# Strassen's seven products for the first layer's down projection, and the branch moved to other banks and hooks

## The chip, the core and the metric

The kernel runs on one core of one Trainium2 chip. The metric is the device time of one launch in microseconds (us), a median over runs. The core has a matrix engine (PE, whose weight loads the profile shows apart as PEld), a vector engine (DVE), an activation engine (ACT), a general engine (POOL) and a queue engine (SP) that starts most of the data transfers (DMA). SBUF is the working memory. PSUM is the small memory that the matrix engine writes to: eight banks of 128 partitions by 512 float32 numbers.

## The reference

Two residual layers act on 2048 tokens of width 512 (two sequences of 1024), all in float32. The part that is changed is layer 0:

```python
xn = layernorm(x)
x = x + attn_ref(xn) + ffn_ref(xn)
# attn_ref: a second layernorm, a recurrence of rank 8 along the sequence,
#           and a small feed-forward of rank 8 behind it ("the branch")
# ffn_ref:
hidden = silu(xn @ W1.T) * (xn @ W3.T)        # 2048 tokens x 2048 hidden
hidden = fwht(hidden)                         # Walsh-Hadamard transform
out = hidden @ W2.T                           # 2048 tokens x 512
```

Layer 1 follows with causal attention of 16 heads and a feed-forward of the same size whose hidden values are thinned to two of every four.

## The kernel before

The Hadamard transform is applied to `W2` once, in SBUF (`fwht_rows`, `fwht_step`), so that layer 0's feed-forward is gate, up and down products alone. The 2048 tokens are four blocks of 512; two blocks are handled together. A *unit* is the gate and the up projection of one pair of blocks for 256 of the 2048 hidden columns: layer 0 has 16 units, `n` 0 to 15, eight for blocks 0 and 1 and then eight for blocks 2 and 3.

`gate_up` (used by both layers) computes a unit by Strassen's algorithm in Winograd's form: seven calls of `products`, each of four matrix products of 128x128 by 128x512, and a few additions. It holds three pairs of PSUM banks, `pa`, `pb` and `pc`; the pairs change roles from unit to unit (`turns`). Between the seven blocks of products it calls `hook(0)` to `hook(6)`. All other work of layer 0 is hung on these hooks: the order of every engine's instructions is the order of the program text (`in_program_order`), and `put0(n, at, f, ...)` says that `f` is issued at hook `at` of unit `n`.

The down projection of a finished unit is not by Strassen. `down(n, i, half)` takes two of the four 128-token rows of block `i`, multiplies with the 256 hidden rows of `W2` into the two remaining PSUM banks (`two_banks`, tags `bank0` and `bank1`), and adds each bank into the residual `x1` on DVE (L634). `some_downs` takes these calls from a list at the hooks, 64 calls in all, from unit 3 on, and what is left comes behind the last unit:

```python
if n >= 3:
    some_downs((1, 1, 1, 1, 1, 1, 2)[at] if n < 5 else (1, 1, 0, 0, 1, 0, 1)[at])
```

The branch of each block is a chain of small steps on the same hooks and the same two banks: `load_again` (x once more, on SP), `branch_scale` (ACT, then POOL), `branch_out` (PE, then DVE L533, then POOL), `branch_add` (DVE statistics, POOL addition into `x1`), then for another block `ln_stats`, `ln_scale`, `ln_turn` (or `next_...`) with transposes on PE; `branch_mlp`, `branch_relu`, `branch_rank` prepare the rank-8 feed-forward, whose product is added inside the bank of the first `down` that comes after it (L628). `branch_scale` and `ln_scale` share one buffer (tag `z`).

Weights for gate and up come in tiles of 512 KB (`load_w13`), five buffers in all. POOL makes their four sums per unit (`combine_w`, L167 to L170), at hook 5 of the unit before.

Layer 1's feed-forward has the same `gate_up`, and its down projection is already by Strassen: for a group of two units and each half of the tokens, DVE makes sums of the hidden values (`down_hidden`, L1250 to L1253), POOL sums of the weights (`down_weights`), PE seven products (`down`, L1316) of four 128x128 by 128x256, and DVE (L1327, L1330), ACT (L1324) and POOL (`add_u2`, L1335) put them together in the residual.

## Time and profile before

| | us |
|---|---|
| Median of 3 runs | 1887.15 (1885.65 to 1887.47) |
| Profiled execution, its own time | 1882.42 |
| Its span in the trace | 1880.5 |
| PE busy | 1822.4 (97%) |
| DVE, POOL, ACT busy | 1067.7, 715.3, 464.8 |
| PE from the first layer-0 `down` to the first layer-1 product | 130.7 to 704.1 |

An entry such as `L621 PE MATMUL acc<-w2h,h ... x512 | 230.1, 594` means: line 621 of the kernel, engine, operation, tile written and tiles read, 512 instructions, 230.1 us busy, 594 ns for one from start to end. Each float32 matrix product of the program stands as two instructions in the trace. Matmuls overlap, so the distance from one to the next, not the length of one, is what a product costs; the chain of waits shows it. Idle time of an engine counts only where PE waits for it.

### The profile page before, as it was taken

The page shows a single profiled execution, that of the slowest core. Times are in us where ns is not written, and L with a number is a line of the kernel's source. Part 1 is how long each engine was busy: PE and PEld are TensorE (multiplying, and loading weights), DVE is VectorE, ACT ScalarE, POOL GpSimd, SP SyncE. Part 2 cuts the span into 40 slices and gives each one's busy share as a digit, 9 for nine tenths or more (in the row PEclk, how much of TensorE's full clock was granted, in tenths as well). Part 3 has the DMA queues.
Part 4 walks back from the last instruction along what each step waited for, and adds up shares of the span by engine and source line. Part 5 has one row for each costly group of instructions (what it writes and reads, how often), then busy time and mean ns, then how long its engine had stood idle before and what let it go on. Part 6 is the DMA issues. An engine that isn't in the chain of part 4 may idle for free.

```text
span 1880.5 us, 17921 instructions
## 1 busy us (share of the span) xinstructions
PE 1822.4 (97%) x6964; PEld 844.2 (45%) x6964; DVE 1067.7 (57%) x1424; ACT 464.8 (25%) x659; POOL 715.3 (38%) x635
## 2 busy tenths in 40 slices
PE   7999999999999999999999999999999999999997
PEld 4444444444444444333333333334455555555553
DVE  3674443334443235656565657652768678668664
ACT  2321121112221102343433343421212211221210
POOL 4222233113432101376667666732243344244310
PEclk9999999999999999999999999999999999999999
DMA  6121111001101100000000100011101102201101
GB/s 236 40 79 34 34 34 34 23 23 34 51 23 34 34 6 23 1 12 12 3 10 12 33 14 1 23 45 34 34 24 55 56 23 79 79 23 50 40 0 45
DMA packets 29459, 68.04 MB, mean 36 GB/s; under 512 B 3392, under 2 KB 11584, under 8 KB 27840
## 3 DMA queue, kind: packets, MB, share of 16 engines
q1 hardware_dynamic: 28656, 66.61, 11.0%
q8 instruction: 55, 0.90, 0.2%
q10 hardware_dynamic: 720, 0.30, 0.1%
q14 instruction: 28, 0.23, 0.0%
HBM read 62.70 MB, written 4.19 MB: 36 GB/s over the span
## 4 chain that ended last, share of the span: by engine, by line
PE 88%; DVE 4%; POOL 4%; ACT 2%; issue 2%; DMA 0%; SPq 0%; ACTq 0%; DVEq 0%; POOLq 0%
PE p_a L177 20%; PE p_c L177 19%; PE acc L621 12%; PE d L1316 8%; PE pq L838 6%; PE m L890 4%; PE s L943 3%; PE o L985 3%; POOL acc L993 3%; PE pv L838 3%; PE dr L1372 2%; PE po L838 2%; PE w L1005 1%; PE pp L480 1%; DVE tops L898 1%
## 5 line engine op out<-in xcount | busy, mean ns | idle before, releaser
L993 POOL TENSOR_TENSOR acc<-acc,pt 128x1024 f32<-128x1024 f32 (+3 forms) x138 | 233.8, 1720 | 0.0
L621 PE MATMUL acc<-w2h,h 128*128 128x512 f32 x512 | 230.1, 594 | 3.1 <-DVE y L533 1.8
L898 DVE TENSOR_REDUCE tops<-m 128x2 f32<-128x1024 f32 (+2 forms) x192 | 180.9, 956 | 49.1 <-PE m L890 44.6
L634 DVE TENSOR_TENSOR x<-x,acc 128x512 f32<-128x512 f32 x128 | 86.1, 685 | 174.5 <-PE acc L621 137.9
L960 ACT ACTIVATE pt<-s 128x1024 f32<-128x1024 f32 (+3 forms) x160 | 115.1, 766 | 180.3 <-PE s L949 164.0
L621 PEld LDWEIGHTS acc<-w2h,h 128*128 128x128 f32 x512 | 96.5, 190 | 123.1 <-issue 115.0
L838 PE MATMUL pq<-xt,wqk 128*128 128x512 f32 x256 | 124.6, 615 | 0.8 <-ACT qk L854 0.8
L177 PE MATMUL p_a<-t_a,s_a 128*128 128x512 f32 x256 | 117.4, 603 | 2.0 <-DVE t_a L154 2.0
L177 PE MATMUL p_a<-xt,w 128*128 128x512 f32 x256 | 118.0, 604 | 0.7 <-ACT xt L134 0.7
L177 PE MATMUL p_c<-xt,s_c 128*128 128x512 f32 x256 | 115.2, 593 | 2.5 <-DVE e_c L221 1.4
L1335 POOL TENSOR_TENSOR x<-x,de 128x512 f32<-128x512 f32 x39 | 62.9, 1628 | 141.7 <-DVE x L1330 120.7
L177 PE MATMUL p_a<-xt,s_a 128*128 128x512 f32 x256 | 115.3, 593 | 0.0
L177 PE MATMUL p_c<-xt,gu 128*128 128x512 f32 x256 | 114.9, 592 | 0.0
L177 PE MATMUL p_c<-t_c,s_c 128*128 128x512 f32 x256 | 114.6, 592 | 0.0
L890 PE MATMUL m<-qk,qk 32*128 32x512 f32 (+3 forms) x768 | 107.5, 533 | 3.6 <-ACT acc L960 3.0
L897 DVE TENSOR_TENSOR m<-m,mask 128x256 f32<-128x256 f32 x128 | 54.7, 428 | 98.5 <-PE m L890 93.9
L943 PE MATMUL s<-qk,qk 32*128 32x512 f32 (+3 forms) x768 | 93.4, 532 | 3.2 <-ACT pt L960 2.3
L177 PEld LDWEIGHTS p_a<-t_a,s_a 128*128 128x128 f32 x256 | 48.7, 193 | 64.0 <-issue 62.4
L177 PEld LDWEIGHTS p_a<-xt,w 128*128 128x128 f32 x256 | 48.5, 193 | 64.3 <-issue 63.0
L965 POOL TENSOR_SCALAR_AFFINE_SELECT pt<-pt 128x256 f32<-128x256 f32 x112 | 48.6, 451 | 69.3 <-ACT pt L960 68.7
L985 PE MATMUL o<-pt,v 128*32 128x512 f32 (+3 forms) x640 | 70.1, 477 | 4.3 <-POOL pt L965 4.0
L838 PEld LDWEIGHTS pq<-xt,wqk 128*128 128x128 f32 x256 | 44.1, 189 | 66.6 <-issue 61.5
(227 smaller groups left out, 2762.1 us busy)
## 6 DMA issues: line engine op xcount, KB each, us to landing
w<-in_W SPq DMA_DIRECT2D x32, 512.0 KB, 3.6
gu<-in_gu SPq DMA_DIRECT2D x32, 512.0 KB, 3.6
wd<-in_down SPq DMA_DIRECT2D x8, 1024.0 KB, 4.9
x<-in_x SPq DMA_DIRECT2D x16, 256.0 KB, 4.2
w2h<-in_W2q SPq DMA_DIRECT2D x4, 1024.0 KB, 11.5
xr<-in_x SPq DMA_DIRECT2D x16, 256.0 KB, 2.6
wqk<-in_WqkvT SPq DMA_DIRECT2D x16, 256.0 KB, 3.2
out_x<-x SPq DMA_DIRECT2D x16, 256.0 KB, 2.0
```

The lines of the kernel that those rows point to most:

```text
L177: nc.tensor.matmul(pair[:, m, :], a[:, m, k, :], x[:, k, :], start=start and k == 0, stop=stop and k == 1, skip_group_check=True,)
L621: nc.tensor.matmul(bank, h[:, m, j * P : (j + 1) * P], w2h[:, :, 2 * (n % NU) + m, :], start=(m == 0), stop=(m == 1 and not up),)
L634: nc.vector.tensor_add(r, r, bank)
L838: nc.tensor.matmul(got[0], lhs(k), rhs(k), start=(k == 0), stop=(k == KC - 1))
L890: nc.tensor.matmul(pair[h // 2][:, h % 2, :e], q[rows, qt * P : (qt + 1) * P], k[rows, c * 512 : c * 512 + e], start=True, stop=True,)
L898: nc.vector.tensor_reduce(out=tops[u][:, c, qt, 2 * p : 2 * p + 2], in_=pair[p][:, :, :e], axis=mybir.AxisListType.X, op=ALU.max,)
L943: nc.tensor.matmul(pair[h // 2][:, h % 2, s:], k[rows, kt * P : (kt + 1) * P], q[rows, cols], start=True, stop=False,)
L960: nc.scalar.activation(pt[:, :, s:], pair[p][:, :, s:], AF.Exp, scale=1.0 / math.sqrt(HD))
L985: nc.tensor.matmul(po[rows, s:], v[:, rows], pts[h // 2][:, h % 2, s:], start=(kt == 0), stop=last, tile_position=(0, h * HD),)
L993: eng.tensor_add(acc[:, :, s:], acc[:, :, s:], pt[:, :, s:])
L1316: nc.tensor.matmul(out_[:, j, :], lhs[:, q, j * P : (j + 1) * P], rhs[:, q, :], start=m in (0, 1, 3, 4) and j == q == 0, stop=j == q == 1, ...
L1335: nc.gpsimd.tensor_add(r, r, held_d["u2"])
```

## The change

Layer 0's down projection is done by Strassen's algorithm as in layer 1, by a shared function, `down_by_seven`. The hidden values of two units lie in one tile (two such tiles). Each group of two units gives, for each half of the tokens, seven `product` calls at the hooks of the next two units, and DVE's `hidden` behind the first of them; one of the four sums overwrites its source (`in_place`). `down_weights` makes the weight sums on POOL; for the second pair of blocks one of them is still in place. The last group comes behind the last unit, its two halves taking turns, with two pairs of PSUM banks besides `bank0` and `bank1`.

The two single banks are now for the down products alone from unit 3 on. The branch takes the third pair, the one of `pb`: `gate_up` asks for `pb` only where it is used, and `two_banks` gives the same pair to the branch before and after it (`one_bank` gives its two halves to the calls of one hook). The steps of the branch are moved to later hooks, `mlp_out` is a step of its own with its own additions, and the branch of block 1 and the preparation of blocks 2 and 3 have other places. Smaller edits: four weight buffers in place of five (so four tiles are loaded at the start in place of five, and unit `n` is followed by the load for unit `n + 2`), two `row` buffers in place of three, the Hadamard matrix in the `rank` tiles, and a smaller scratch area.

```diff
-        pa, pb, pc = (ps_pair(f"p{m}_{name}", (turns + m) % 3) for m in range(3))
+        pa, pc = (ps_pair(f"p{m}_{name}", (turns + m) % 3) for m in (0, 2))
...
         def other_half():
+            pb = ps_pair(f"p1_{name}", turns % 3)
             products(pb, w1[:, :, 2:, :], x[:, 2:, :], start=True, stop=True)
             nc.vector.tensor_add(e[0], e[0], pb)
...
+    def down_by_seven(pool, hs, td, quarters_w, first_block, in_place=False):
+        sd, banks, e1, u2 = {}, {}, {}, {}
+        def quarters_h(n, half):
+            h = hs[n].rearrange("p (q two) b n -> p q two b n", two=2)
+            js = slice(half * TT // 2, (half + 1) * TT // 2)
+            return [h[:, :, c, i, js] for i in range(2) for c in range(2)]
...
+        def hidden(n, half, tags=("sd2", "sd3", "sd4")):
+            h11, h12, h21, h22 = quarters_h(n, half)
+            s3, s4 = (half_tile(tag, f"{tag}_{n}_{half}") for tag in tags[1:])
+            s2 = h11 if in_place else half_tile(tags[0], f"sd2_{n}_{half}")
+            sd[n, half] = s2, s3, s4
+            nc.vector.tensor_sub(s3, h11, h21)
+            nc.vector.tensor_add(h21, h21, h22)
+            nc.vector.tensor_sub(s2, h21, h11)
+            nc.vector.tensor_sub(s4, h12, s2)
...
+        def product(n, half, m, bank=None, tags=("de1", "de2")):
+            h11, h12, s1, h22 = quarters_h(n, half)
+            w11, t3, w21, w22 = quarters_w(n)
+            s2, s3, s4 = sd.get((n, half), (None,) * 3)
+            t1, t2, t4, t3 = (td[n] + [t3])[:4]
+            lhs, rhs = (
+                (h11, w11), (s2, t2), (h12, w21), (s1, t1), (s3, t3), (s4, w22), (h22, t4)
+            )[m]
+            if m in (0, 1, 3, 4):
+                if bank is None:
+                    bank = ps_bank(f"d{m}_{n}_{half}", (m + half) % 2)
+                banks[half, m % 2] = bank
+            out_ = banks[half, m % 2].rearrange("p (j d) -> p j d", j=2)
+            for j in range(2):
+                for q in range(2):
+                    nc.tensor.matmul(
+                        out_[:, j, :], lhs[:, q, j * P : (j + 1) * P], rhs[:, q],
+                        start=m in (0, 1, 3, 4) and j == q == 0, stop=j == q == 1,
+                        skip_group_check=True,
+                    )
+            if m == 0:
+                e1[half] = half_tile(tags[0], f"de1_{n}_{half}")
+                nc.scalar.copy(e1[half], out_)
+            elif m == 1:
+                u2[half] = half_tile(tags[1], f"de2_{n}_{half}")
+                nc.vector.tensor_add(u2[half], e1[half], out_)
+            else:
+                r = residual(n, half, *((0, 0), (1, 1), (1, 1), (0, 1), (1, 0))[m - 2])
+                nc.vector.tensor_add(r, r, out_)
+        def add_u2(n, half, *quarters):
+            for q in quarters:
+                r = residual(n, half, *q)
+                nc.gpsimd.tensor_add(r, r, u2[half])
+        def products_of(n, half):
+            for m in range(7):
+                yield product, n, half, m
+                if m == 1:
+                    yield add_u2, n, half, (0, 1), (1, 0)
+                if m == 4:
+                    yield add_u2, n, half, (1, 1)
+        return hidden, product, products_of
...
-            pool, tag, bufs = (res, "wqk", 2) if m % 5 in (2, 3) else (a, "w13", 3)
-            w13[m] = pool.tile([P, 2, KC, P], F32, tag=tag, name=f"w13_{m}", bufs=bufs)
+            pool, tag = (a, "w13") if m // 2 % 2 else (res, "wqk")
+            w13[m] = pool.tile([P, 2, KC, P], F32, tag=tag, name=f"w13_{m}", bufs=2)
...
             nc.sync.dma_start(out=w2h[:, q], in_=t["W2q"][q])
-            if q < 3:
+            if q < 2:
...
-            return a.tile([P, D], F32, tag="row", name=name, bufs=3)
+            return a.tile([P, D], F32, tag="row", name=name, bufs=2)
...
         def two_banks(name):
-            return [ps_bank(f"{name}_{n}", n) for n in range(2)]
-        turn = 0
+            if now < (3, 0):
+                return [ps_bank(f"{name}_{n}", n) for n in range(2)]
+            pair = ps_pair(name, turns % 3)
+            return [pair[:, n, :] for n in range(2)]
...
         def one_bank(name):
+            if now not in shared:
+                shared[now] = two_banks(name)
+            return shared[now].pop(0)
...
-            nxt = a.tile([P, P], F32, tag="had", name=f"had{step}", bufs=2)
+            nxt = a.tile([P, TT], F32, tag="rank", name=f"had{step}", bufs=2)[:, :P]
...
-        h0, downs = {}, []
-        def down(n, i, half):
-            h, js = h0[n, i], (2 * half, 2 * half + 1)
-            up = i in hf_t and (i, half) not in joined
-            if up:
-                joined.add((i, half))
-            banks = two_banks(f"acc_{n}_{i}_{half}")
+        def mlp_out(i, half):
             for bank, j in zip(banks, js):
-                for m in range(2):
-                    nc.tensor.matmul(
-                        bank, h[:, m, j * P : (j + 1) * P], w2h[:, :, 2 * (n % NU) + m, :],
-                        start=(m == 0), stop=(m == 1 and not up),
-                    )
-            if up:
-                for bank, j in zip(banks, js):
-                    rows = slice(32 * j, 32 * j + R + 1)
-                    nc.tensor.matmul(
-                        bank, hf_t[i][rows, j * P : (j + 1) * P], wup_aug[rows, :],
-                        start=False, stop=True,
-                    )
+                rows = slice(32 * j, 32 * j + R + 1)
+                nc.tensor.matmul(
+                    bank, hf_t[i][rows, j * P : (j + 1) * P], wup_aug[rows, :],
+                    start=True, stop=True,
+                )
             for bank, j in zip(banks, js):
                 r = x1[i][:, j, :]
                 nc.vector.tensor_add(r, r, bank)
-        joined = set()
-        def some_downs(n):
-            for _ in range(min(n, len(downs))):
-                down(*downs.pop(0))
...
+        def quarters_w(n):
+            return [w2_quarters[:, n % (NU // 2), c, e] for c in range(2) for e in range(2)]
+        def down_weights(n, m):
+            w11, w12, w21, w22 = quarters_w(n)
+            if m == 0:
+                td[n] = [
+                    a.tile([P, 2, D // 2], F32, tag=f"td{k}", name=f"td{k}_{n}") for k in (1, 2, 4)
+                ]
+            t1, t2, t4 = (v.rearrange("p q (s d) -> p q s d", s=2) for v in td[n])
+            if m == 0:
+                if n < NU // 2:
+                    nc.gpsimd.tensor_sub(w12, w22, w12)
+                nc.gpsimd.tensor_add(t2, w12, w11)
+            elif m == 1:
+                nc.gpsimd.tensor_sub(t1, w22, t2)
+            else:
+                nc.gpsimd.tensor_sub(t4, w21, t2)
+        down_hidden, down, products_of = down_by_seven(
+            a, h0, td, quarters_w, lambda n: n // (NU // 2) * 2, in_place=True
+        )
...
-            between.setdefault((n, at), []).append(what)
+            between.setdefault((n + at // 7, at % 7), []).append(what)
+        for n in range(NU - 1):
+            u = 2 * n + 2
+            places = [range(7), range(7, 14)]
+            if n == 0:
+                places = [(7, 8, 8, 9, 9, 10, 10), (11, 12, 12, 13, 13, 14, 14)]
+            elif n == 1:
+                places = [range(1, 8), (8, 9, 10, 11, 12, 13, 13)]
+            for half, at in enumerate(places):
+                for f, *args in products_of(n, half):
+                    if f == down:
+                        place = at[args[2]]
+                    put0(u, place + (f != down), f, *args)
+                    if f == down and args[2] == 0:
+                        put0(u, place, down_hidden, n, half)
+            for m, (k, f) in enumerate(((1, 1), (3, 1), (6, 1))):
+                at = places[1][k] + f
+                put0(u, at, down_weights, n + 1, m)
+        put0(2, 5, down_weights, 0, 0)
+        put0(2, 6, down_weights, 0, 1)
+        put0(2, 6, down_weights, 0, 2)
...
-            ((NU, 0), (NU, 2), (NU, 3)), ((NU, 3), (NU, 5), (NU, 6)),
+            ((6, 6), (7, 4), (7, 5)), ((8, 4), (8, 5), (8, 6)),
...
         for base in (0, NU):
             i, d = 2 * base // NU, base + (1 if base else 3)
             for m in range(4):
                 k = i + m // 2, m % 2
-                put0(d + m - 1, 6, load_again, *k)
-                put0(d + m, 0, branch_scale, *k)
-                put0(d + m, 2, branch_out, *k)
-                put0(d + m, 3, branch_add, *k)
+                put0(d + m, 0, load_again, *k)
+                put0(d + m, 2, branch_scale, *k)
+                put0(d + m, 3, branch_out, *k)
+                put0(d + m, 4, branch_add, *k)
                 k = (2 if base == 0 else 0) + m // 2, m % 2
-                put0(d + m, 3, next_stats if base else ln_stats, *k)
-                put0(d + m, 4, next_scale if base else ln_scale, *k)
-                put0(d + m, 5, next_turn if base else ln_turn, *k)
-            for m in range(2):
-                for at, f in ((0, branch_mlp), (1, branch_relu), (3, branch_rank)):
-                    put0(d + 2 * m + 2, at, f, i + m)
+                put0(d + m, 2, next_stats if base else ln_stats, *k)
+                put0(d + m, 5, next_scale if base else ln_scale, *k)
+                put0(d + m, 7, next_turn if base else ln_turn, *k)
+        for i, steps in enumerate((
+            ((5, 4), (5, 5), (6, 4), (6, 5), (8, 4)), ((7, 4), (7, 6), (8, 3), (9, 4), (10, 4)),
+            ((11, 4), (11, 5), (12, 4), (12, 5), (13, 4)),
+            ((13, 3), (13, 5), (14, 3), (14, 4), (14, 5)),
+        )):
+            for k, n in enumerate(steps):
+                if k < 3:
+                    put0(*n, (branch_mlp, branch_relu, branch_rank)[k], i)
+                else:
+                    put0(*n, mlp_out, i, k - 3)
...
-            put0(NU - 2, 3 + 3 * half, branch_in, 2, half)
-            put0(NU - 1, 1 + 2 * half, branch_in, 3, half)
-            put0(NU - 2 + half, 5, ln_spread, 2 + half)
+            put0(5 + half, 4, branch_in, 2, half)
+            put0(7, 3 + 2 * half, branch_in, 3, half)
+            put0(5 + half, 5, ln_spread, 2 + half)
...
-            for m in range(2):
-                h0[n, i0 + m] = a.tile(
-                    [P, 2, TT], F32, tag="h0", name=f"h0_{n}_{i0 + m}", bufs=6
-                )
+            if n % 2 == 0:
+                h = h0[n // 2] = a.tile([P, 4, 2, TT], F32, tag="h0", name=f"h0_{n}", bufs=2)
...
-                if n >= 3:
-                    some_downs((1, 1, 1, 1, 1, 1, 2)[at] if n < 5 else (1, 1, 0, 0, 1, 0, 1)[at])
...
-            downs += [(n, i0 + i, half) for i in range(2) for half in range(2)]
-            for m in (2 * n + 5, 2 * n + 6):
+            for m in (2 * n + 4, 2 * n + 5):
                 if m < 4 * NU:
...
-        some_downs(len(downs))
+        for f, *args in between.pop((2 * NU, 0), ()):
+            f(*args)
+        n, second_half = NU - 1, list(products_of(NU - 1, 1))
+        for step in products_of(n, 0):
+            for f, *args in (step, second_half.pop(0)):
+                if f == down and args[1] and args[2] in (0, 1, 3, 4):
+                    if args[2] in (0, 3):
+                        pair = ps_wide(f"d{args[2]}_{n}")
+                    f(*args, pair[:, args[2] in (1, 4), :], ("e2", "e3"))
+                else:
+                    f(*args)
+                if f == down and args[2] == 0:
+                    down_hidden(n, args[1], *([("", "e1", "t1")] if args[1] else []))
...
+        down_hidden, down, products_of = down_by_seven(
+            c_, hs, td, quarters_w, lambda n: 2 * units[2 * n][0]
+        )
...
+    nc = bacc.Bacc(
+        "TRN2", target_bir_lowering=False, num_devices=1, dynamic_dma_scratch_size=1024
+    )
```

## The prediction

> **What bounds the kernel now.** I read the page first. Its busy times say that PE is the engine to look at:
>
> ```profile
> PE 1822.4 (97%) x6964; PEld 844.2 (45%) x6964; DVE 1067.7 (57%) x1424; ACT 464.8 (25%) x659; POOL 715.3 (38%) x635
> ```
>
> That is an average, so next the windows of the stage that changes, from the first layer-0 down product to the first product of layer 1 (length, then PE, PEld, DVE, ACT, POOL busy, clock, DMA share, GB/s):
>
> ```profile
> 130.70:704.10 573.40, 570.33 (x1482) 257.55 (x1481) 224.51 (x390) 101.81 (x141) 147.38 (x124) 1.00 0.10 30
> ```
>
> PE is busy for 570 of 573 us at full clock; DVE has 39%, POOL 26%, DMA 10%. So what PE no longer does comes off the time, provided nothing makes it wait. The chain of waits, in order of time, gives the price of PE's work. First layer 0, then layer 1, whose down projection has the new form already:
>
> ```profile
> 134.29 3.43 PE p_a L177 x8
> 137.72 3.43 PE acc L621 x8
> ...
> 686.96 17.17 PE acc L621 x40
> 704.13 15.64 PE pq L838 x36
> ```
>
> ```profile
> 1355.39 1.73 PE d L1316 x8
> 1357.12 3.43 PE p_c L177 x8
> 1360.55 1.73 PE d L1316 x8
> ```
>
> Eight instructions with 512 columns take 3.43 us, eight with 256 take 1.73. Layer 1 repeats block and product every 5.16 us, so its interleaving leaves no gap there. Last, the groups of operations that will be exchanged, with shapes kept apart: DVE and POOL in layer 0, then in layer 1.
>
> ```profile
> L634 DVE TENSOR_TENSOR x<-x,acc 128x512 f32<-128x512 f32 x128 | 86.1, 685 | 174.5 <-PE acc L621 137.9 <-PE acc L628 36.7
> ...
> L545 POOL TENSOR_TENSOR x<-x,y 128x512 f32<-128x512 f32 x16 | 20.0, 1271 | 0.0
> ```
>
> ```profile
> L1330 DVE TENSOR_TENSOR x<-x,d 128x512 f32<-128x512 f32 x65 | 44.5, 684 | 46.9 <-PE d L1316 46.9
> ...
> L1250 DVE TENSOR_TENSOR sd<-h 128x512 f32<-128x512 f32 x13 | 13.8, 1059 | 0.0
> ...
> L1252 DVE TENSOR_TENSOR sd<-h 128x512 f32<-128x512 f32 x13 | 9.0, 692 | 0.4
> ```
>
> ```profile
> L1335 POOL TENSOR_TENSOR x<-x,de 128x512 f32<-128x512 f32 x39 | 62.9, 1628 | 141.7 <-DVE x L1330 120.7 <-DVE de L1327 21.1
> ...
> L1231 POOL TENSOR_TENSOR td<-wd 128x512 f32<-128x512 f32 x7 | 14.8, 2111 | 0.0
> ```
>
> **What the Trainium skill says.** "TensorE: Matmul & The Clock Gate", Back-to-back issue gap, has the gap between matmuls grow with the columns and almost no fixed part (its figures are for bf16). The trace agrees on the proportion: 3.43/8 = 0.429 and 1.73/8 = 0.216 us. Each product needs its own weight load, 190 ns in the trace, still under 216. "SBUF — State Buffer", section "SBUF: two separate sides", has DVE and POOL exclude each other for a whole instruction when DVE reads two operands from SBUF. The trace fits: L1250 takes 1059 ns where L1252, of the same shape, takes 692, and POOL additions range from 1271 to 2111.
>
> **The change, part by part.**
>
> 1. *Down products on PE.* Removed: 64 calls of 3.43 us = 219.6. Added: 8 groups x 2 halves x 7 products = 112 of 1.73 = 193.8. Minus 25.8 us, all on the path.
>
> 2. *The branch's feed-forward output* (`mlp_out`): the same 16 matrix products, no longer joined to a down call. PE 0; 16 more DVE additions of 0.685 = 11 us.
>
> 3. *DVE.* Removed 128 x 0.685 = 88. Added per half: four `hidden` operations at layer 1's lengths (1.06 + 0.69 + 0.69 + 1.09), one sum of 0.69, five residual additions of 0.684: 7.6 us, times 16 = 122. With part 2 DVE gets 45 us more, 270 in about 550 us: 49%. Hidden behind PE's blocks as long as each is in time. The critical one is s2, the third operation of `hidden`, for product 1. For most halves product 0 is at hook 0. Count from the end of block 7: PE does product 6 to 1.7, block 1 to 5.2, product 0 to 6.9, block 2 to 10.3, then product 1. DVE has its addition from `pc` at 1.4, the residual at 2.6, the last `h` at 3.3, two subtractions at 5.1, and s2 after product 0 at about 7.8. Slack 2.5 us: cost 0. In unit 3 the second half starts at hook 4, behind an addition of 1.22 and one of 0.68: s2 at 5.7 after block 5, product 1 wanted at 5.15. Cost 0.6, up to 2 if POOL holds DVE.
>
> 4. *ACT:* 16 copies of 0.58 = 9 us. One place matters: block 6 follows block 5 with one product (1.73) between, and needs ACT's copy of 1.01 from the same banks. Layer 1 runs exactly this. Cost 0.
>
> 5. *POOL.* 48 `add_u2` of 1.63 = 78 and 28 weight sums at 1.26 to 2.11, say 1.7, = 48: 273 in 550 us, 50%. The busiest are branch units: unit 5 has 17 additions and three short powers, about 25 to 28 us in 39. PE waits for POOL only at the second block of the next unit (`combine_w`); following POOL's order through units 5 and 9, its first sum is done some 8 us ahead. Cost 0.
>
> 6. *The third pair.* A `branch_out` at hook 3 needs the pair that `pb` had just left: DVE's addition ends about 1.45 us after block 4, the product between lasts 1.73. The two statistics of hook 2 (each 0.67 + 0.18, rows L113 and L114) end before. Slack 0.3 us, eight times. `mlp_out`, `branch_rank` and `ln_turn` come a hook or more after the pair's last user. Cost 0; 1.4 each if a statistic lies in between.
>
> 7. *DMA and SP.* Both weight tiles of unit n + 2 are asked for after unit n and wanted at hook 5 of the next, some 25 us; a 512 KB load lands in 3.6. The 16 loads of `load_again` stand between them in SP's queue and wait for row buffers freed in the unit before; two hooks (10 us) against 2.6. At the start one tile less is loaded ahead. Cost 0.
>
> 8. *The tail.* Before: five down calls, 17.17 us, no gap. After: one product of group 6, then 14. They are counted in part 1, but the cover is gone: the last `h` is ready only 3.3 us after block 7. s2 of the first half comes at 5.5 (PE free at 5.15), that of the second at 8.3 (PE free at 7.2). Cost 1.5, from 0.5 to 4. Layer 1's first products read older tiles and wqk, loaded earlier: nothing queues there.
>
> Sum: -25.8 + 0.6 + 1.5 = **-23.7 us**. The layer-0 stretch goes from 573.4 to 549.7, the span from 1880.5 to about 1857, the profiled execution from 1882.42 to 1859. The median of the runs stands 4.7 above that execution, so 1887.15 - 23.7 = 1863.4.
>
> **Rivals.**
>
> *A, small waits add up.* The `branch_out` slack of 0.3 us is lost eight times at 1.4 (11 us), or DVE is held at hook 1 for some halves. For it: the narrow slack, and L1250's spread. Against: layer 1's last stage has more DVE load (414 us of the 609 from its first gate product, 68%), and its down products waited for DVE's `h` 1.8 us in all. Gain 9 to 19: 1868 to 1878.
>
> *B, POOL becomes the bound, slower.* In units 4 to 6 and 9 to 12 POOL has some 18 additions plus powers in a unit. One such unit takes PE 7 x (3.43 + 1.73) and some 2.7 us of transposes and branch products, 39 us, and POOL 18 x d + 1.5, so it decides from d = 2.08 us; above that PE waits at block 2 of every such unit. The saving is gone at 3.4 us over in each of the seven units, d = 2.27. At 2.6, 18 x 2.6 + 1.5 = 48, 9 over, times seven = 63: 1887 - 24 + 63 = 1926. For it: L1231 took 2.11. Against: layer 0's POOL rows lie at 1.27 to 1.52, and layer 1's mean over all its rows is 197/127 = 1.55.
>
> *C, the saving is hidden anyway.* That would need another engine on the path; 570 of 573 us of PE speak against it. 1887.
>
> **How the numbers follow.** Likeliest 0.75 (1859 to 1868), A 0.15, B 0.05, C 0.02, and 0.03 for a larger gain from gaps before unit 3 that close (1855 to 1859). A measurement of this kernel can't tell less than about 0.2% (3.8 us) from no change. Faster: 0.75 + 0.15 + 0.03, less 0.02 for an A that eats it all: 0.91. Same: C and half of that 0.02: 0.03. Slower: B and the other half: 0.06. The predicted time is the likeliest's, 1863.4. The lower end is 25.8 us without any wait, less the runs' spread of 1.5: 1859, taken to 1858. The upper takes in half of A: 1873.
>
> **What would show it.** 896 instructions of the seven products with 256 columns, eight in 1.73 us, in place of 512; PE idle in the layer-0 stretch under 6 us; layer 1 unchanged in length (1176 us from its first product to the end); DVE near 49% and POOL near 50% in the stretch; a PE wait of about 1 us for a `sd` or `h` subtraction in the tail. Wrong if PE shows repeated waits for DVE at hooks 1 or 3, or for `combine_w`, or if 256-column products that read W2 in pieces of 128 columns take over 0.216 us: 0.24 would cost 896 x 0.024 = 22 us, nearly the whole gain. (The old `down` read `w2h` in the same pieces at 3.43 per eight, the price of any block.)

## The result, and the profile after it

The changed kernel takes 1892.77 us (median of six runs, 1891.04 to 1895.18); the kernel before, beside it, took 1885.21 (1883.86 to 1887.47). The ratio is 1.0040, with a 95% interval of 1.0027 to 1.0053: slower by 7.6 us, where 24 us less were forecast. The profiled execution has a span of 1889.3 us against 1880.5.

From the page of the changed kernel, the busy line and the chain's shares by engine:

```profile
PE 1809.9 (96%) x7348; PEld 922.7 (49%) x7348; DVE 1129.1 (60%) x1472; ACT 474.9 (25%) x675; POOL 819.5 (43%) x711
...
PE 84%; DVE 7%; POOL 4%; ACT 2%; issue 2%; DMA 1%; SPq 0%; DVEq 0%; ACTq 0%; POOLq 0%
```

PE does less than before (1809.9 us instead of 1822.4), in 384 more instructions: 896 of the new form in place of 512, as forecast. But the span grew, and DVE now has 7% of the chain that ended last. Next the window from the first layer-0 down product to the first product of layer 1 (length, then PE, PEld, DVE, ACT, POOL busy, clock, DMA share, GB/s):

```profile
131.94:714.57 582.63, 556.65 (x1866) 335.66 (x1865) 287.59 (x439) 111.99 (x157) 249.56 (x200) 0.98 0.10 31
```

This stretch was 573.4 us long before and should have become 549.7. It is 582.6, so 32.9 us over the forecast. What follows it takes 1174.7 us (1176.4 before), what stands ahead of it 131.9 (130.7): the whole error lies in the stretch, and this one line divides it. PE's idle time is 582.6 - 556.7 = 26.0 us; the forecast had 5.2 (3.1 as before, 0.6 in unit 3 and 1.5 in the tail), so 20.8 us are waits. PE's busy time should have been 570.3 - 25.8 = 544.5 and is 12.1 us more, and the clock column says why: 0.98, where it was 1.00. The waits of PE by line, over the same window (us in total, times, the longest), name the first part, 26.0 us in all:

```profile
PE pt_d L131 <- DVE xt L136: 10.3, 4, 3.2
PE pt_a L131 <- DVE xt L136: 5.8, 4, 1.9
PE d L290 <- DVE h L265: 5.2, 4, 3.1
PE ph L575 <- DVE low L663: 3.3, 1, 3.3
PE pu L575 <- ACT rank L561: 0.7, 1, 0.7
PE pu L654 <- ACT rank L561: 0.7, 1, 0.7
```

The largest item, 16.1 us, is not a product waiting for its operand. It is a transpose (`L131`) that waits for the copy (`L136`) of other transposes, eight times, once in each half block of `ln_turn` and `next_turn`. The chain of waits shows one of them, in unit 10:

```profile
441.64 1.65 DVE sd L263
...
443.32 1.66 DVE h L264
...
445.07 1.57 DVE h L265
...
446.67 0.69 DVE sd L266
447.36 0.61 DVE xt L136
...
448.11 1.09 PE pt_d L131 x4
449.19 4.37 PE p_a L177 x8
```

Read it from below. The second four transposes start at 448.11, because only then has DVE copied the first four, which PE had done by 445.0. The copy takes 0.6 us but stands behind all four operations of `hidden` (`L263` to `L266`). From unit 3 on `two_banks` returns the two halves of one pair, and a pair is one tile: `transpose_row` writes the first half, its copy reads it, and the next `transpose_row` writes the same tile again, so it is made to wait for that read although it touches the other bank. Before, each row had a bank tile of its own.

The last line shows the second part of the loss. Eight products of gate and up take 4.37 us here instead of 3.43. The windows of this place, with the granted clock behind POOL's column:

```profile
449.19:453.57 4.38, 4.38 (x10) 1.91 (x9) 0.00 (x0) 0.59 (x1) 0.00 (x0) 0.80 0.00 0
453.57:458.70 5.13, 5.13 (x17) 3.01 (x17) 0.69 (x1) 0.00 (x0) 2.49 (x2) 1.00 0.00 0
```

PE is busy throughout the first window, at 0.80 of its clock, and back at 1.00 in the second. Five such blocks stand in the stretch, one behind each of the five waits of 2.26 us or more: 4.37, 5.09, 5.13 and 6.04 us for eight products of 512 columns (3.43) and 5.19 for sixteen of 256 (3.45). Together that is 8.7 us, and sixteen small products of `branch_in` behind the 3.3 us wait, which stand ahead of the block of 6.04, lose another 1.6. The rest of the 12.1, 1.8 us, I have not assigned to rows.

Last two of the groups that answer to those shown of before, with shapes kept apart:

```profile
L308 POOL TENSOR_TENSOR x<-x,de 128x512 f32<-128x512 f32 x48 | 62.1, 1308 | 165.7 <-DVE de L300 114.3 <-DVE x L303 35.6 <-DVE x L716 15.8
...
L263 DVE TENSOR_TENSOR sd<-h 128x512 f32<-128x512 f32 x15 | 17.4, 1161 | 0.2
```

The load of DVE in the stretch is as forecast, 287.6 of 582.6 us, and POOL's is lower, 249.6. The four operations of `hidden` take 3.86 us together where 3.53 had been assumed, in the mean; they are not all alike, as an experiment below shows. No engine became the bound.

### The profile page after: what moved, and what is told of

It is laid out like the page before. It is cut to its first block, busy times and chain, and to the rows that moved or that the text cites. A ratio compares the mean times of both kernels' runs of the same rounds, so it can differ in the third digit from the quotient of the medians.

```text
span 1889.3 us, 18906 instructions
## 1 busy us (share of the span) xinstructions
PE 1809.9 (96%) x7348; PEld 922.7 (49%) x7348; DVE 1129.1 (60%) x1472; ACT 474.9 (25%) x675; POOL 819.5 (43%) x711
## 4 chain that ended last, share of the span: by engine, by line
PE 84%; DVE 7%; POOL 4%; ACT 2%; issue 2%; DMA 1%; SPq 0%; DVEq 0%; ACTq 0%; POOLq 0%
PE p_a L177 19%; PE p_c L177 19%; PE d L290 18%; PE pq L984 6%; PE m L1036 4%; PE s L1089 3%; PE o L1131 3%; POOL acc L1139 3%; PE po L984 3%; PE dr L1452 2%; PE pv L984 2%; PE w L1151 1%; ACT acc L1106 1%; DVE tops L1044 1%; PE s L1095 1%
## 5 line engine op out<-in xcount | busy, mean ns | idle before, releaser
L308 POOL TENSOR_TENSOR x<-x,de 128x512 f32<-128x512 f32 x87 | 125.0, 1451 | 307.4 <-DVE x L303 156.2
L303 DVE TENSOR_TENSOR x<-x,d 128x512 f32<-128x512 f32 x145 | 99.4, 686 | 158.4 <-PE d L290 158.1
L290 PE MATMUL d<-td,h 128*128 128x256 f32 x592 | 141.4, 383 | 5.2 <-DVE h L265 5.2
L290 PEld LDWEIGHTS d<-td,h 128*128 128x128 f32 x592 | 113.2, 192 | 49.5 <-issue 30.2
L177 PE MATMUL p_a<-t_a,s_a 128*128 128x512 f32 x256 | 123.6, 629 | 2.1 <-DVE t_a L154 2.1
L170 POOL TENSOR_TENSOR s_c<-gu,s_c 128x512 f32<-128x512 f32 x16 | 20.4, 1276 | 134.2 <-PE p_c L177 134.2
```

The source lines that it names most:

```text
L177: nc.tensor.matmul(pair[:, m, :], a[:, m, k, :], x[:, k, :], start=start and k == 0, stop=stop and k == 1, skip_group_check=True,)
L290: nc.tensor.matmul(out_[:, j, :], lhs[:, q, j * P : (j + 1) * P], rhs[:, q], start=m in (0, 1, 3, 4) and j == q == 0, stop=j == q == 1, sk ...
L303: nc.vector.tensor_add(r, r, out_)
L308: nc.gpsimd.tensor_add(r, r, u2[half])
```

## The experiments

The expectations call PE TensorE, DVE VectorE and POOL GpSimd, and some speak of a run that is shown further down but was made before. Their letters are not those of the prediction's rivals. The theory (A): PE waits within a step, for reads of the half of a pair that was written first; the DVE queue makes these waits long; the clock falls behind the long ones. The rivals: DVE or POOL is late with layer 0's work as a whole, so that PE must wait for it somewhere (B); or moving the branch costs more than such waits, whatever form the down projection has (C). "Stretch" is again the time from the first down product to layer 1's first product.

### All transposes ahead of the copies

`transpose_row` gets a `part`: 0 for the transposes, 1 for the copy.

```diff
-    def transpose_row(dst, src, j, bank, act):
+    def transpose_row(dst, src, j, bank, act, part=None):
         pt = bank.rearrange("p (k c) -> p k c", c=P)
-        for k in range(KC):
-            nc.tensor.transpose(pt[:, k, :], src[:, k * P : (k + 1) * P], ident)
+        if part != 1:
+            for k in range(KC):
+                nc.tensor.transpose(pt[:, k, :], src[:, k * P : (k + 1) * P], ident)
+        if part == 0:
+            return
...
-            for m, bank in enumerate(two_banks(f"pt_d{i}_{half}")):
-                transpose_row(xt1[i], z[:, m, :], 2 * half + m, bank, m)
+            banks = two_banks(f"pt_d{i}_{half}")
+            for part in range(2):
+                for m, bank in enumerate(banks):
+                    transpose_row(xt1[i], z[:, m, :], 2 * half + m, bank, m, part)
...
```

`ln_turn` is changed in the same way from unit 3 on.

> Edit: from unit 3 on, all eight transposes of a half block are issued before the two copies that read them; the work is otherwise that of the changed kernel. Theory A (the pair of banks is one tile, so the second four transposes wait for the copy of the first four, and that copy stands on VectorE behind the four `hidden` operations): the waits of TensorE in front of transposes for the copy, 16.1 us in the changed kernel (10.3 for `pt_d`, 5.8 for `pt_a`), fall to under 1 us, and three blocks of gate products that ran at a lower clock behind them (4.37, 5.09 and 5.13 us instead of 3.43) come back, 4.3 us. Together 20 us: the time falls from 1892.8 to 1871-1875. Theory B (VectorE or GpSimd is simply late with the work of layer 0, and TensorE must wait for it somewhere): the same 16 us appear in front of another instruction (a product of the down projection or of gate and up), and the time stays at 1888-1893.

Measured: 1872.87 us (1868.19 to 1876.36), ratio to before 0.9929 (0.9906 to 0.9953). The stretch is 560.9 us, 21.6 less. The two waits of `L131` are gone from the list; every other wait in the stretch is there with its old length, and no new one has come. B is refuted for these 16 us: DVE and POOL do the same work in the same order as in the changed kernel. The three slow blocks behind these waits are back at their full clock. One block, at 300.2, that had it in the changed kernel took 5.38 us here.

### The copy ahead of `hidden`

```diff
+                steps = between.pop((n, at), [])
+                if n >= 3:
+                    turn_steps = [x for x in steps if x[0] in (ln_turn, next_turn)]
+                    hid = [k for k, x in enumerate(steps) if x[0] == down_hidden]
+                    if turn_steps and hid:
+                        steps = [x for x in steps if x not in turn_steps]
+                        steps[hid[0] : hid[0]] = turn_steps
-                for f, *args in between.pop((n, at), ()):
+                for f, *args in steps:
                     f(*args)
```

> Edit: at the hooks that hold both, the turn of a half block (transposes, copy, transposes, copy) is issued ahead of the four `hidden` operations, so that the copies stand before them on VectorE. The pair stays one tile. Theory A: each of the eight waits falls to the length of a copy with its signals, about 1.0 us as in units 4 and 5, where `hidden` stands a hook later: 16.1 becomes about 8 us, and without long waits the clock holds (4.3 us): about 12 us, so 1879-1883. `hidden` comes about 2 us later, and where it is then late for the second product a wait of up to 1 us each in five units shows in front of a product of the down projection: 1879-1886 with it. Theory B (VectorE or GpSimd late as a whole): no change, 1888-1893, with the waits moved.

Measured: 1879.44 us, ratio 0.9969 (0.9955 to 0.9983), stretch 569.3. The waits of the run, over layer 0:

```profile
PE d L290 <- DVE h L265: 5.2, 4, 3.1
PE pt_a L131 <- DVE xt L136: 3.9, 4, 1.1
PE pt_d L131 <- DVE xt L136: 3.5, 4, 0.9
```

16.1 us became 7.4, 0.88 to 1.1 each, and the blocks behind all eight have their full clock. That is the bare price of a copy between two writes of one tile. The other half of the 16.1 was the queue in front of the copy. `hidden`, now later, made no product wait: the first line is unchanged. So the slack that the forecast had found for `hidden` was there, in these units.

### How long `hidden` takes

In nine of the sixteen halves of the changed kernel each operation of `hidden` takes 0.69 us. In the other seven (both of unit 3, and one each in units 6 and 10 to 13) one to four of them take 1.2 to 1.8 us, in unit 10 the first three 1.6 each; there POOL was at work beside them. One POOL operation is moved away:

```diff
-            for m, (k, f) in enumerate(((1, 1), (3, 1), (6, 1))):
+            for m, (k, f) in enumerate(((1, 1), (3, 1), (6, 4 if n < NU - 2 else 1))):
```

> Edit: the changed kernel with one step moved on GpSimd alone: the third weight sum (`t4`) of each next group three hooks later, so that it doesn't run beside `hidden`. Theory A: `hidden` took 1.6 us an operation instead of 0.69 where GpSimd ran beside it (two sums of the unit's weights, then `t4`); without `t4` beside it its third operation falls from 1.56 to 0.69 in unit 10 and its fourth from 1.63 to 0.69 in unit 12, and the waits of the transposes behind it (3.15 and 3.17 us) fall by about 0.9 us each, with part of the clock lost behind them; the waits of units 6, 7, 11 and 13 stay within 0.2 us. Time 1888-1892. Theory B (TensorE's waits do not hang on how long `hidden` takes): the two waits stay within 0.2 us.

Measured: 1889.56 us (3.2 less than the changed kernel), ratio 1.0028 (1.0019 to 1.0037), stretch 577.9. The chain of waits in unit 10 of this run:

```profile
438.65 1.65 DVE sd L263
...
440.33 1.65 DVE h L264
...
442.07 0.70 DVE h L265
...
443.49 0.61 DVE xt L136
...
444.24 0.63 PE pt_d L131 x4
```

The third operation fell from 1.57 to 0.70, and the wait behind it from 3.15 to 2.25 us; in unit 12 from 3.17 to 2.23. The others stayed within 0.2 us. So in these two units each 0.9 us that POOL's presence adds to `hidden` is 0.9 us of PE's wait. The first two operations are still slow, beside two sums of the unit's weights. "SBUF — State Buffer", section "SBUF: two separate sides", of the Trainium skill says that DVE with two operands from SBUF and a POOL operation that reads SBUF exclude each other; this run agrees, 0.70 against 1.57 us with nothing else changed at that place. The blocks behind the two shorter waits are still slow, 5.13 us each; those of units 3 and 11, behind waits as long as before (3.08 and 2.26 us), had their full clock in this trace.

### Two smaller waits, one at a time

The branch's first projection ahead of its last, at the hook that they share:

```diff
+        for half in range(2):
+            put0(5 + half, 4, branch_in, 2, half)
         for i, steps in enumerate((
             ((5, 4), (5, 5), (6, 4), (6, 5), (8, 4)), ((7, 4), (7, 6), (8, 3), (9, 4), (10, 4)),
...
         for half in range(2):
-            put0(5 + half, 4, branch_in, 2, half)
             put0(7, 3 + 2 * half, branch_in, 3, half)
```

> Edit: at hook 4 of units 5 and 6 the branch's first projection (of blocks 2) is issued ahead of its last one (of blocks 0), with which it shares a pair; nothing else. Theory A: the projection no longer waits for VectorE's read `low` of the other half of the pair (3.3 us at 254.7), its sixteen products take 2.0 instead of 3.6 us, and the gate products behind them lose 1.8 instead of 2.6 us to the clock, as in the run with all four orders: 5.5 to 6 us, 1886-1888. Theory B (the wait moves to another instruction of the branch): under 2 us, 1891-1894.

Measured: 1888.64 us, ratio 1.0017 (1.0003 to 1.0031), stretch 578.4: 4.1 us less, not 5.5 to 6. The wait is gone, but the gate products behind the two runs of small products took 6.6 us, no less than in the changed kernel. This loss does not hang on the wait alone.

The second half of the first group's products, later:

```diff
-                places = [(7, 8, 8, 9, 9, 10, 10), (11, 12, 12, 13, 13, 14, 14)]
+                places = [(7, 8, 8, 9, 9, 10, 10), (11, 13, 13, 14, 14, 15, 15)]
```

> Edit: of the first group's second half, products 1 to 6 come at hooks 13, 13, 14, 14, 15, 15 instead of 12, 12, 13, 13, 14, 14, so that one hook lies between `hidden` and the first product that reads it; nothing else. Theory A: the wait of 3.1 us for `hidden` at 168.1 goes, with the 1.6 us of the slow products behind it: 4 to 5 us, 1888-1889. Against it: the later products may run into the second group's first ones at unit 4's hook 1, where two more products then stand and their residual additions with them: then 1890-1892.

Measured: 1890.46 us, ratio 1.0025 (1.0016 to 1.0034), stretch 578.6: 3.9 us less there, about the least expected, but only 2.3 less in the median, which lies in the range of the expectation's other case. What that case named, a wait of the later products, is not in the trace: the 3.08 us wait and its slow block are gone, and no other wait came. A block at 300.4, which had its full clock in the changed kernel, took 5.38 us.

### All four orders together

The edits of the four runs that change the order on PE and DVE in one kernel: transposes ahead of copies, turn ahead of `hidden`, `branch_in` first, second half later. The weight sum stays where it was.

> Edit: four changes of order together: all eight transposes before the copies, the turn ahead of `hidden`, the branch's first projection ahead of its last at the hook that they share (hook 4 of units 5 and 6), and the second half of the first group's products one or two hooks later (hooks 6 of unit 3 on, with one hook between `hidden` and the product that reads it). Theory A (waits within a step, and the clock lost behind them, are all that the forecast missed): the 27 us of TensorE's waits in layer 0 fall to 4 us or less and the 8.7 us of slow blocks to under 1: the time falls by 28 to 32 us, to 1861-1866, close to the forecast of 1863.4 and below the kernel before (1885.2). Theory B (VectorE or GpSimd late as a whole): 1885-1893. Between, 1867-1880: theory A in part, and what is left is to be read from the waits.

Measured: 1860.47 us (1857.66 to 1863.32), ratio to before 0.9865 (0.9847 to 0.9883). It beats both kernels. The window of its stretch, and its waits (in this kernel the line numbers from `transpose_row` on are three higher or more):

```profile
131.95:681.13 549.18, 545.84 (x1865) 330.70 (x1864) 276.38 (x439) 111.84 (x157) 246.88 (x200) 1.00 0.11 33
```

```profile
PE d L293 <- DVE h L268: 2.1, 3, 0.9
...
```

The forecast's stretch was 549.7 us and its time 1863.4. With the waits taken out, by order alone, both hold. Unit 10's place in its chain now reads:

```profile
425.42 1.73 PE d L293 x8
427.15 0.87 PE pt_d L132 x8
428.02 3.44 PE p_a L180 x8
```

Eight transposes pass without a stop, and the block behind them has its full clock.

### Two further orders

To the four orders are added `branch_in` of blocks 2 at hook 1 of units 5 and 6, with a pair of its own, and the weight sum three hooks later as above.

```diff
         for half in range(2):
-            put0(5 + half, 4, branch_in, 2, half)
+            put0(5 + half, 1, branch_in, 2, half)
```

> Edit: the run with all four orders, and two more: the branch's first projection of blocks 2 at hook 1 of units 5 and 6 (alone, with its own pair) instead of at the hook that it shares, and the third weight sum (`t4`) on GpSimd three hooks later, away from `hidden`. Theory A: the block of gate products behind the two runs of small products (5.38 us at 246.1) comes back to 3.6 us and the 0.3 us waits for `low` go, 2 us in all: 1857-1861. If the new hook has nothing to cover the projection's read, a wait of about 1 us each shows there and nothing is gained: 1860-1862.

Measured: 1856.91 us (1851.92 to 1860.16), ratio 0.9860 (0.9843 to 0.9876), stretch 546.6, at the lower edge of what was expected. The block of 5.38 us that was left behind the small products, at 246.1, is gone with the two waits of 0.3 us. That the new hook brought it back is not shown: in the last two runs of the next section the same small products stand at the shared hook as in the run with the four orders, and the block behind them has its full clock all the same. Against the four orders alone the intervals overlap.

### The branch moved alone

The other half of the change: the branch in its new banks, hooks and order, with the down projection of before (`whole_down` is the old `down` without the branch's own product).

```diff
-        for n in range(NU - 1):
-            u = 2 * n + 2
...
+        def whole_down(n, i, half):
+            banks = [ps_bank(f"acc_{n}_{i}_{half}_{k}", k) for k in range(2)]
...
                 for f, *args in between.pop((n, at), ()):
                     f(*args)
+                if n >= 3:
+                    some_downs((1, 1, 1, 1, 1, 1, 2)[at] if n < 5 else (1, 1, 0, 0, 1, 0, 1)[at])
```

> Edit: the branch in its new banks, hooks and order, and the second pair taken late, all as in the changed kernel, but the down projection as before (four whole products of a block half, two banks, the old pace; `mlp_out` separate), without `hidden`, without the weight sums and without the sums on GpSimd. Theory A: the moved branch carries a wait of its own: eight times about 1.0 us (a copy between two sets of transposes in one tile), and up to 3.3 us where two steps share a pair at one hook; the copies stand behind nothing long, so few waits reach the 3 us behind which the clock fell: 8 to 12 us slower than before, 1893-1897. The down projection by seven is then worth its 25.8 us, of which the order behind `hidden` took back 8 and the clock 4 to 9. Theory C (the move costs nothing, all loss is of the sevenfold projection): within 2 us of before, 1883-1887.

Measured: 1927.75 us, ratio 1.0227 (1.0205 to 1.0248), stretch 616.1. 30 us above what A expected, and 40 above C. The chain of waits in unit 5 shows what A had left out:

```profile
262.30 1.23 DVE e_a L202
...
263.58 1.13 PE pe L623 x4
264.70 5.34 PE p_a L177 x8
```

`branch_out` at hook 3 takes the pair that gate and up have just left, and DVE must first have read it (`L202`). The forecast's step 6 had found that a down product covers this read; in this kernel the down products stand behind the branch's steps, and nothing covers it: twelve waits of 1.4 us, 16.7 in all, with slow blocks behind some.

Next the downs ahead of the steps:

```diff
+                if n >= 3:
+                    some_downs((1, 1, 1, 1, 1, 1, 2)[at] if n < 5 else (1, 1, 0, 0, 1, 0, 1)[at])
                 for f, *args in between.pop((n, at), ()):
                     f(*args)
-                if n >= 3:
-                    some_downs((1, 1, 1, 1, 1, 1, 2)[at] if n < 5 else (1, 1, 0, 0, 1, 0, 1)[at])
```

> Edit: as the run with the branch moved and the old down projection, but at each hook the down products stand ahead of the branch's steps, as the products of the sevenfold form do in the changed kernel; there they stood behind. Theory A (what that run lost is that nothing covered the read of the third pair, which gate and up leave only when VectorE has added it): its twelve waits of 1.4 us for `e_a`, 16.7 us, and the slow blocks behind them, 9 us, go; the waits inside a pair stay (7.0 us at the transposes, 3.3 to 4.4 us at the shared hook with 2 to 5 us of clock, up to 3.4 us for `rank`): 1895-1903. Theory C (the move itself costs more, wherever the products stand): over 1915.

Measured: 1917.43 us (1914.99 to 1918.98), ratio 1.0172 (1.0155 to 1.0190), stretch 605.8: 14 us above A's range, and within C's. Ten of the twelve waits remain. The pace puts no down product at hook 3 from unit 5 on, so only units 3 and 4 were covered: an error in my expectation, which leaves open whether C is right.

With all transposes ahead of their copies, and `branch_in` first at the shared hook (the two edits shown above):

> Edit: as the run with the old down projection ahead of the branch's steps, with two of the four orders besides: all eight transposes before their copies, and the branch's first projection ahead of its last at the shared hook. Theory A (waits within one step are all that moving the branch costs): the time is that of the kernel before within 4 us, 1883-1889, and against the run with all four orders (1860.5) it leaves 22 to 28 us as the worth of the down projection by seven, where the forecast had 25.8 less a tail of 1.5. Theory C: a loss of over 10 us remains, 1895 or more.

Measured: 1905.16 us (1904.11 to 1907.91), ratio 1.0112 (1.0097 to 1.0127), stretch 594.7. The waits at the transposes and at the shared hook are gone, and the ten uncovered reads are still there, 13.9 us, with five slow blocks of 1.8. By its number this speaks for C, by its waits for A; the last run of the row decides:

```diff
-                    some_downs((1, 1, 1, 1, 1, 1, 2)[at] if n < 5 else (1, 1, 0, 0, 1, 0, 1)[at])
+                    some_downs((1, 1, 1, 1, 1, 1, 2)[at] if n < 5 else (1, 0, 0, 1, 1, 0, 1)[at])
```

> Edit: as the mended run with the old down projection, with one further change of its pace: from unit 5 on the four down products of a unit stand at hooks 0, 3, 4 and 6 instead of 0, 1, 4 and 6, so that one covers VectorE's read of the third pair at hook 3 in every unit. Theory A (all that moving the branch costs are waits within one step and uncovered reads): the ten waits of 1.4 us for `e_a` (13.9 us) and the five slow blocks behind them (9.0 us) go, so 1905.2 becomes 1880-1887, the time of the kernel before; against the run with all four orders (1860.5) the down projection by seven is then worth 20 to 27 us. Theory C (the move costs more): 1892 or more.

Measured: 1882.56 us (1880.11 to 1886.59), ratio to before 0.9994 (0.9987 to 1.0001), and the window of its stretch:

```profile
131.18:702.18 571.00, 569.75 (x1481) 257.39 (x1480) 238.77 (x406) 101.72 (x141) 146.18 (x124) 1.00 0.11 31
```

One down product of each unit moved from hook 1 to hook 3 is worth 22.6 us in the median. C falls: the branch in its new place costs nothing that can be measured once each read is covered and no step waits within itself; with neither it cost 43 us. Against the two runs with the sevenfold products in order, the stretch differs by 21.8 and 24.4 us, the median by 22.1 and 25.7: that is what the down projection by seven is worth here, where the forecast had 23.7.

## Why the prediction was wrong, step by step

The step that failed is the sixth; the third had one size wrong, and the sum had no term for the clock. PE's 26.0 us of waits are, rounded, 19.4 of step 6, 3.4 in unit 3, 1.7 in the tail and 1.4 for `rank`.

1. *Down products.* Right. Eight take 1.73 us also where they read W2 in pieces of 128 columns, and PE's busy time in the run with all further orders is 543.84 us against 570.33 of before: 26.5 us less, where 25.8 were forecast. The price in proportion to the columns is the trace's. The formula that the prediction cites from the Trainium skill ("TensorE: Matmul & The Clock Gate", section "Back-to-back issue gap") is for a single product; the sustained figures of that section, 81 ns for 128 columns and 131 for 512, are not in proportion to the columns as these are, and the measurement decides.

2. *The branch's output.* Right: its 16 DVE additions took 10.2 us.

3. *DVE.* The slack at hook 0 was right: no product waits for s2 in units 4 to 13, even with the copy in front of `hidden`. Two things were missed. Unit 3's second half was sized at 0.6 us, up to 2 if POOL holds DVE, and measured 3.1 plus a slow block of 1.7; its first half waited for another 0.4. The chain of waits has DVE's work in front of that product (the operation ahead of these, `L197`, took 1.75):

```profile
163.86 1.68 DVE sd L263
...
165.56 1.65 DVE h L264
```

From 162.0 to 166.7 POOL makes three sums of the unit's weights (`L167` to `L169`). Where POOL is not beside them, the three operations of DVE take 2.05 us together; here they took 5.08. The difference, 3.0 us, is nearly the whole wait. It is an estimate from this trace and the run with the weight sum moved; no run moved these three sums. And the step asked only what waits for `hidden`, not what is queued behind it on DVE: the copy that half a step of transposes needs.

4. *ACT*, 5. *POOL*, 7. *DMA.* Right: no block of gate products in the stretch waits for `combine_w`, for ACT's copy or for a load. POOL's additions took 1.31 us, not 1.63, and its share is 43%, not 50%. ACT's `rank` cost two waits of 0.7 us, which no step had.

6. *The third pair.* This step failed, in its sentence "`mlp_out`, `branch_rank` and `ln_turn` come a hook or more after the pair's last user. Cost 0". It compared each step with the user of the pair before it. But from unit 3 on the pair has two users within the step: the first half's copy and the second half's transposes, or two steps of the branch at one hook. Measured: 16.1 us in eight turns, with 4.3 us of slow blocks behind three of them, and 3.3 us at the shared hook, with 2.6 in the slow block and 1.6 in the small products behind it. Issuing the transposes first took the 16.1 us away, and 19.9 us of the median. The narrow slack of 0.3 us at hook 3, which the step did examine, held all eight times; and the runs with the branch alone show it worth examining.

8. *The tail.* Right in its sum, 1.7 us where 1.5 stood; its parts were 0.35 and 1.1 and came out as 0.85 and 0.88.

The sum had no term for the clock. It took 1.00 over, as the whole stretch of before shows it, where PE never waited for more than 0.9 us. But the profile of before has the price in layer 1's last stage, outside that stretch. A wait of 2.63 us is followed by eight products of 512 columns in 5.38 us, and one of 1.92 us by eight at full clock:

```profile
1840.87 5.38 PE dr L1372 x8
...
1860.55 3.71 PE dr L1372 x8
```

So a wait's further cost, 1.7 us at times, could be seen there, though not when it falls due.

Of the prediction's rivals, A had the right kind (several waits for DVE, none large) in the wrong places, with 9 to 19 us left of the gain. Rival B, the one on the slower side, did not occur. The forecast said that it would be wrong if PE waited for DVE again and again at hooks 1 or 3; it did at hook 0.

## What to carry to other kernels

When buffers are merged into a larger tile, ask of each tile not only who used it last, but who uses it twice within one step: a write of one part waits for the read of another. Issue all writes before the first read, and put a short copy that PE wants ahead of long work on its engine. Keep a product between the last use of a buffer and its next: one down product in each unit, moved to where it covers a read, was worth 22.6 us. And price a wait of PE at more than its length, since the products behind it may run slower too: here eight waits of 16.1 us cost 20.

## What the runs showed of the hardware

The clock's dependence on short waits was not expected. The table counts the larger groups of waits of PE in all 13 traces, and how often the products behind them were slow, which cost 1.0 to 3.0 us each. Where no transposes or small products are named, ordinary products of 256 or 512 columns stand on both sides.

| PE waits, us | where | times | slow |
|---|---|---|---|
| 3.31 to 4.44 | ahead of small products, at the shared hook | 6 | 6 |
| 3.13 to 3.18 | between transposes | 6 | 6 |
| 3.07 to 3.08 | for `hidden` in unit 3 | 5 | 4 |
| 2.59 to 2.63 | layer 1, last stage | 13 | 6 |
| 2.23 to 2.27 | between transposes | 6 | 5 |
| 1.92 | layer 1, last stage | 13 | 4 |
| 1.76 to 1.89 | between transposes | 12 | 0 |
| 1.51 | layer 1, first down product | 13 | 7 |
| 1.38 to 1.39 | ahead of four products with ten rows | 20 | 11 |
| 0.87 to 1.11 | between transposes | 32 | 0 |
| 0.84 to 0.89 | for `hidden` in the tail | 16 | 0 |

Of the waits above 3 us 16 of 17 slowed what followed, of those under 1.2 us in the table none. In between the length does not decide: in layer 1, which does the same work in all runs, a wait of the same length at the same place cost 1.7 us in some traces and nothing in others. "TensorE: Matmul & The Clock Gate", section "HAM oscillation — how this bites in real kernels", of the Trainium skill warns of idle gaps above about 3.4 us; here waits of 1.5 us between ordinary products were followed by a lower clock in 7 of 13 cases, so the measurements decide. Whether transposes count as idle time is not shown.

A block behind small products can be slow with hardly a wait. In the run with all four orders PE waits for 0.3 us only, yet the block behind two runs of narrow products is slow; its timeline:

```profile
243.06 1.86 PE L583 MATMUL pp<-wp,xt 128*128 128x24 f32 x16
245.21 1.06 PE L662 MATMUL pp<-woa,ht 128*128 128x8 f32 x8 [0.29 <-ACT low L587]
246.12 5.38 PE L180 MATMUL p_a<-t_a,w 128*128 128x512 f32 x8
```

The run with `branch_in` first has the same sequence and a slow block as well; the last two runs of the branch alone have it with a full clock. The blocks at 300.2 and 300.4 noted above stand behind a wait of 0.7 us and sixteen small products, and other traces have them at full clock. What decides, where the length of the wait does not, stays open.
